# Reordering a four-layer image kernel: the last three blocks, attention in rounds of eight, and the first stage's orders

## The chip, the cores and the metric

The kernel runs on one core of a Trainium2 chip. The metric is the device time of one execution in microseconds (us); the time before is 2684.59 us, the median of three runs (2683.01 to 2685.78). All data are float32. The engines of the core are TensorE (PE, with PEld for its weight loads), VectorE (DVE), ScalarE (ACT), GpSimd (POOL) and SyncE (SP), which issues the DMAs.

## The reference

Four layers follow one another on `x`, 4 images of 512 channels and 64 x 64 pixels:

```python
# layer 0: attention over the 4096 pixels, 64 channels each for key, query, value
t = einsum('oc,bchw->bohw', w_qkv, x)                 # key_, query, value = thirds of t
attn = softmax(einsum('bdk,bdq->bkq', key_, query), axis=1)
x = scale * einsum('oc,bchw->bohw', w_out, einsum('bdk,bkq->bdq', value, attn)) + x
# layer 1: 1x1, 3x3 and 1x1 convolutions, weights mixed from 8 experts per image
rw = sigmoid(x.mean(axis=(2, 3)) @ router_w.T + router_b)
x = relu(bn3(conv(relu(bn2(conv(relu(bn1(conv(x, rw.w1))), rw.w2))), rw.w3)) + x)
# layer 2: linear attention with softplus features
Q, K, V = softplus(Wq x + bq), softplus(Wk x + bk), Wv x + bv
x = x + gamma * (Q (K V)) / (Q . (sum(K) + EPS))
# layer 3: two projections, one scanned along rows and then columns, gating the other
g, s = split(w_proj x + b_proj)
s = ds_cumsum(ds_cumsum(s, discount, axis=2), discount, axis=3)   # y_t = d*y_{t-1} + x_t
x = x + gamma * g * sigmoid(s)
```

## The kernel before, in words

**Layout.** An image is held as four pairs of pixel blocks (`NPAIR` = 4), each pair 128 partitions x 4 channel groups x 1024 pixels, in `xs[0]` to `xs[3]`; a fifth place (`places[NPAIR]`) serves as scratch. The images are worked one after the other: `layer0` to `layer3` for `b` in 0 to 3. SBUF and PSUM tiles come from pools with a number of buffers per tag: pairs of PSUM banks (`pair_psum`, tag `s`) have 3 buffers, single banks (`bank`, tag `acc`) 2, `four` 6, `block` 7. A new tile waits until the buffer that it takes has been read for the last time.

**What sets the order.** TensorE's instructions keep the order of the program everywhere (`manual_schedule` for PE around the loop over images). In the first stage VectorE and ScalarE keep it too, in the attention loop ScalarE alone, and in layer 3 VectorE and ScalarE. Where an engine is not named, a planner orders its instructions by the dependencies and its own estimates. The DMAs are all issued by SP.

**First stage of layer 0 (`Projections`).** Keys and queries of two pairs at a time come from a scheme with seven products instead of eight, each of them two accumulating matmuls per half (four pairs of matmuls in the trace). Steps are named in the strings that `steps` returns. A digit is a product: 1, 6, 7, 4 accumulate in one bank `y` (kq), 2 and 3 and 5 in a pair `zy` (kqz); product 3 writes the half of `zy` that 5 began. `seed` copies `y` after product 1 into `zy`, `e2` and `e3` copy `y` after 6 and 7 into SBUF (ScalarE), so that the next product in `y` waits for that copy. `c11` makes four copies of `zy` into the keys (ScalarE, L290), `c22` adds `zy` and `e3` into the queries (VectorE, L326), `c21` copies and `c12` adds (VectorE, L324, L318). `k` copies keys of the pair that `c12` made to the other half of the partitions (ScalarE, L290). `t5`, `t6`, `n5` and so on are differences of `x` (VectorE, L252, two instructions each): `t` for this pair of pairs, `n` for the next one, which are the terms of products 5, 6, 7 and 4. `v0` to `v3b` are the products for the values (`vv`, L260), `cp` copies these (L266), `tr` turns them on TensorE (L273) and copies the result on VectorE (L277). Image 0 has a string of its own, since its `x` is still being loaded: `wqkv_sb`, the parameters and then the blocks of `x` are the first DMAs on SP's queue, the other weights follow, and GpSimd scales two of them (L119, L120). At the head of `layer0` a preload of the exponential's activation table stands on ScalarE (L342).

**Attention.** 128 steps per image: 4 blocks of queries (`pr`), 32 blocks of keys each (`kt`). `scores(i)` is two pairs of matmuls into a pair of banks (L365), an exponential on ScalarE into one of twelve ring buffers (L368) and an addition on VectorE that sums the exponentials (`acc`, L371 and L373). `values(i)` is two pairs of matmuls from the ring buffer (L380). The loop goes by groups of six: scores of group g, then what is due of `late` (at most two entries), then values of group g - 1; in the first group there are no values, so its scores and those of the second follow each other, with `key_copies` and, in image 0, the transposes of `router_of_values` (with a copy on VectorE, L173) in between. `late` holds, for a finished block of queries, `sums` (den on TensorE, L396; a reciprocal, a product and two reductions on VectorE) and, for the first two blocks, four `out_step`s: `y` on TensorE (L424) into a pair of banks, `add_out` on VectorE (L429). The last den is in group 21, before the values of step 124. `pool` adds ScalarE work in eight of the groups (L442).

**Layer 3.** Eight tiles per image: 4 pairs by 2 pairs of channel groups. A tile has two blocks, `Sums` (the scanned projection) and `Gates` (the gate), each of seven products with the same scheme (`x` a single bank, `zy` a pair; L919). A loop over i takes `s` = sums of tile i, `g` = gates of tile i - 1, and `l` = the scans of the sums of tile i - 1, in the interleaved order of the tuples `steps`; `first_steps` serves i = 0, `last_steps` i = 8, where only the gates of tile 7 are left. `rows` scans along rows (VectorE, two instructions, L952), `turn` transposes within the partition (ScalarE, L958), `columns` adds the carry and scans (VectorE, L965, L969), `sigmoid` ends it (ScalarE, L975), `d` sets the factors of the next column scan (ScalarE, L885). `seed` and `copy_out` are ScalarE's copies as above (L924, L928). In `Gates`, `first` and `third` multiply a half tile (VectorE, L980, L987), `fourth` and `second` add and multiply (L983, L988, L992, L993); `third` and `second` end with `add_x`, which adds `x` over 1024 columns (L998) and issues one write of 512 KB on SP (L999). Between the blocks stand parts of the next image's first stage (`t`, `v`, `x`), where there is a next image.

Of the kernel before, what the change touches and what calls it, by code (L numbers as in the profile page):

```python
# [15 lines left out]
P = 128  # L16
# [20 lines left out]
RING = 12  # L37

# [7 lines left out]
def unshifted(ctx: ExitStack, tc: tile.TileContext, fits, x, wqkv_t, wout_t, router_t,  # L46
# [165 lines left out]
    class Projections:  # L212
# [16 lines left out]
        def steps(self, b):  # L229
            first = "v1 cp01 5 1 seed v2 t6 t4 n5 6 n6 e2 2 7 e3 c11 c22 tr01 n7 4 c21 3 c12 n4"  # L230
            if b == 0:
                first = "zero v0 1 seed t5 v1 cp01 t6 5 2 t7 t4 6 e2 v2 7 e3 c11 c22 tr01 n5 n6 n7 4 c21 3 c12 n4"
            return first.split(), "5 1 seed k v3a 6 e2 2 v3b cp23 7 e3 c11 c22 tr23 4 c21 3 c12".split()
# [105 lines left out]
    def layer0(b, xs, pro):  # L339


        tc.keep_in_program_order(nc.scalar.preload_act_table_set("natural_log_exp_and_others"))  # L342
# [6 lines left out]
        with tc.manual_schedule(engines={mybir.EngineType.DVE, mybir.EngineType.Activation}):  # L349
            pro.sum_weights()  # L350
            for pair, steps in zip(((0, 1), (2, 3)), pro.steps(b)):
                pro.products(xs, pair, steps, key, qry, vt)
        ringx = places[NPAIR].rearrange("p i (h n) -> p i h n", h=2)
# [89 lines left out]

        groups = [range(i, min(i + RING // 2, NPAIR * NT)) for i in range(0, NPAIR * NT, RING // 2)]
        late = []
        with tc.manual_schedule(engines={mybir.EngineType.Activation}):
            for g, group in enumerate(groups):
                for i in group:
                    scores(i)
                if 1 < g < 2 + 2 * KC:  # L450
                    pool(NPAIR - 2 + (g - 2) // KC, (g - 2) % KC)
                if g == 0:
                    pro.key_copies()
                    if b == 0:
                        router = router_of_values()
                    continue
                for _ in range(2):
                    if late and late[0][0] < g:
                        late.pop(0)[1]()
                for n, i in enumerate(groups[g - 1]):  # L460
                    if g == len(groups) - 1 and n == 4:
                        inverse_sums(NPAIR - 1)
                    pr = values(i)
# [4 lines left out]
                if b == 0 and g == 1:  # L468
                    router()
        assert not [t for t in late if t[0] < len(groups) - 1], late  # L470
# [16 lines left out]
        for i in groups[-1]:  # L487
            values(i)
# [378 lines left out]
    def layer3(b, xs, value_product, value_add, left, weights, wcq):  # L867
# [109 lines left out]
        class Gates(Block):  # L977
            def first(self):
                s = self.half(0, 0)
                nc.vector.scalar_tensor_tensor(s, self.zy[:, 0, :], self.bias[0], s, ALU.add, ALU.mult)  # L980

            def fourth(self):
                nc.vector.tensor_tensor(self.e[3], self.zy[:, 1, :], self.e[3], ALU.add)  # L983

# [549 lines left out]
```

## Time and profile before

| | |
|---|---|
| median of 3 runs | 2684.59 us (2683.01 to 2685.78) |
| profiled execution | 2685.98 us, its span 2684.2 us |
| TensorE busy | 2648.0 us, 99% of the span |
| VectorE busy | 2013.3 us, 75% |
| ScalarE busy | 1314.3 us, 49% |
| GpSimd busy | 12.1 us |
| DMA | 115.16 MB, mean 43 GB/s |
| first scores of images 0 to 3 | 57.30, 722.78, 1386.39, 2050.00 us |

The profile is one execution taken by the hardware profiler; times count from the start of its span. Idle time on an engine that is not the one that sets the pace costs nothing by itself. TensorE's matmuls are pipelined: two that use different halves of the array start within 0.01 us of each other, so pairs are what is counted here, and their spacing (0.43 us for 512 columns) tells more than their duration (about 0.6 us). The profile's stated idle time before an instruction counts from the end of the one before. The granted clock is the share of full speed that TensorE was given.

### The profile page before, as it was taken

Reading aid. Unit: us, or ns where it says so; the run is one execution under the profiler, and the core shown is the slowest. Engines: PE = TensorE matmul, PEld = TensorE weight load, DVE = VectorE, ACT = ScalarE, POOL = GpSimd, SP = SyncE. Lnnn points to the kernel's source line nnn. Section 1 sums busy time; section 2 is a strip of 40 time slices with the busy share of each in tenths; the row PEclk is TensorE's granted clock in tenths of the full one; section 3 lists DMA queues with packets and bytes.
Section 4 is the critical chain, followed back from the end, with each engine's and each line's share of the span. In section 5 each row is a group of like instructions: output and inputs, shape, how many; then the busy total and the mean of one; then the engine's idle time right before and its main releaser. Section 6 shows DMA issues by size and latency. Waiting matters only on the chain.

```text
span 2684.2 us, 25782 instructions
## 1 busy us (share of the span) xinstructions
PE 2648.0 (99%) x10048; PEld 1112.5 (41%) x10048; DVE 2013.3 (75%) x2270; ACT 1314.3 (49%) x1510; POOL 12.1 (0%) x26
## 2 busy tenths in 40 slices
PE   8999999999999999999999999999999999999998
PEld 2333364344333346434433334543443333554443
DVE  5688766788778876688877778668886787856787
ACT  3654353545565535345456553535555645363545
POOL 1000000000000000000000000000000000000000
PEclk9999999999999999999999999999999999999999
DMA  5000210021200021002220002101121000210011
GB/s 191 1 1 1 102 32 1 16 110 71 87 1 1 1 102 32 1 29 97 79 79 1 0 1 102 32 1 63 63 94 63 0 1 1 102 32 1 32 47 48
DMA packets 34594, 115.16 MB, mean 43 GB/s; under 512 B 2976, under 2 KB 12192, under 8 KB 32928
## 3 DMA queue, kind: packets, MB, share of 16 engines
q1 hardware_dynamic: 34464, 113.43, 11.4%
q8 instruction: 81, 1.33, 0.2%
q14 instruction: 49, 0.40, 0.1%
HBM read 79.86 MB, written 33.55 MB: 42 GB/s over the span
## 4 chain that ended last, share of the span: by engine, by line
PE 90%; DVE 5%; ACT 4%; issue 1%; DMA 0%; SPq 0%; DVEq 0%; ACTq 0%
PE av L380 17%; PE s L365 16%; PE sx L919 14%; PE zy L919 10%; PE z L663 4%; PE c L638 4%; PE c L566 4%; PE c L615 3%; PE wv L837 2%; PE y L424 2%; PE g L739 2%; PE xtr L724 2%; PE vv L260 2%; PE c2e L615 2%; PE kqz L304 1%; PE kq L304 1%
## 5 line engine op out<-in xcount | busy, mean ns | idle before, releaser
L365 PE MATMUL s<-qv,key 64*128 64x512 f32 x2048 | 463.9, 598 | 4.3 <-ACT x L368 3.1
L373 DVE TENSOR_TENSOR acc<-acc,ring 128x1024 f32<-128x1024 f32 x312 | 381.6, 1223 | 97.4 <-ACT ring L368 69.5
L368 ACT ACTIVATE ring<-s 128x1024 f32<-128x1024 f32 x336 | 317.1, 1038 | 211.0 <-PE s L365 211.0
L380 PE MATMUL av<-ring,qv 128*64 128x512 f32 x1344 | 304.5, 595 | 0.0
L365 PEld LDWEIGHTS s<-qv,key 64*128 64x128 f32 x2048 | 189.1, 186 | 276.2 <-issue 173.6
L373 DVE TENSOR_TENSOR acc<-acc,x 128x1024 f32<-128x1024 f32 x168 | 205.5, 1223 | 99.8 <-ACT x L368 86.6
L368 ACT ACTIVATE x<-s 128x1024 f32<-128x1024 f32 x176 | 172.0, 1041 | 181.9 <-PE s L365 181.9
L919 PE MATMUL sx<-t,x 128*128 128x512 f32 x512 | 238.1, 599 | 1.4 <-ACT e L928 0.8
L380 PEld LDWEIGHTS av<-ring,qv 128*64 128x64 f32 x1344 | 93.2, 137 | 198.7 <-issue 198.7
L380 PE MATMUL av<-x,qv 128*64 128x512 f32 x704 | 167.1, 597 | 0.0
L924 ACT COPY zy<-sx 128x512 f32<-128x512 f32 x64 | 36.5, 570 | 265.9 <-PE sx L919 256.3
L969 DVE TENSOR_TENSOR_SCAN t<-x,t 128x512 f32<-128x512 f32 x128 | 149.1, 1209 | 1.5
L919 PEld LDWEIGHTS sx<-t,x 128*128 128x128 f32 x512 | 94.6, 190 | 132.6 <-issue 121.1
L958 ACT COPY t<-s 128x1024 f32<-128x1024 f32 x64 | 127.5, 1992 | 41.9 <-DVE s L952 41.4
L952 DVE TENSOR_TENSOR_SCAN s<-wc,s 128x512 f32<-128x512 f32 x128 | 145.9, 1201 | 0.0
L928 ACT ACTIVATE e<-sx,prm_sb 128x512 f32<-128x512 f32 x128 | 86.9, 686 | 107.0 <-PE sx L919 107.0
L975 ACT ACTIVATE s<-t 128x1024 f32<-128x1024 f32 x64 | 125.6, 1988 | 12.1 <-DVE t L969 12.0
L919 PE MATMUL sx<-t,wq 128*128 128x512 f32 x256 | 117.0, 597 | 2.1 <-ACT e L928 2.1
L919 PE MATMUL zy<-t,wq 128*128 128x512 f32 x256 | 118.2, 602 | 0.0
L919 PE MATMUL sx<-x,wq 128*128 128x512 f32 x256 | 117.1, 595 | 0.0
L919 PE MATMUL zy<-x,x 128*128 128x512 f32 x256 | 116.2, 594 | 0.0
L663 PE MATMUL z<-x,wqk_sb 128*64 128x512 f32 x512 | 115.8, 597 | 0.0
(228 smaller groups left out, 3445.8 us busy)
## 6 DMA issues: line engine op xcount, KB each, us to landing
out_dram<-s SPq DMA_DIRECT2D x64, 512.0 KB, 2.6
x<-in_x_dram SPq DMA_DIRECT2D x14, 2048.0 KB, 8.7
ex<-in_packed_dram SPq DMA_DIRECT2D x4, 2048.0 KB, 7.5
ex<-in_experts_dram SPq DMA_DIRECT2D x4, 2048.0 KB, 7.8
wq<-in_wproj_t_dram SPq DMA_DIRECT2D x32, 256.0 KB, 5.1
ex<-in_packed_dram SPq DMA_DIRECT2D x4, 1536.0 KB, 6.2
ex<-in_experts_dram SPq DMA_DIRECT2D x4, 1536.0 KB, 6.8
x<-in_packed_dram SPq DMA_DIRECT2D x4, 1536.0 KB, 8.2
```

What stands on the lines that cost most here:

```text
L365: nc.tensor.matmul(s[:, h, :], key[r, kt * P:(kt + 1) * P], qry[r, pr * NB:(pr + 1) * NB], start=True, stop=True)
L368: nc.scalar.activation(p, s, AF.Exp)
L373: nc.vector.tensor_tensor(accs[pr], accs[pr], p, ALU.add)
L380: nc.tensor.matmul(avs[pr][h * D:(h + 1) * D, :], vt[:, kt, :], ring[i % RING][:, h, :], start=kt == 0, stop=kt == NT - 1)
L566: nc.tensor.matmul(y[:, h, :], wc[:, kc, :], xs[pr][:, kc, h * NB:(h + 1) * NB], start=kc == 0, stop=kc == KC - 1)
L615: nc.tensor.matmul(y[:, lo - a:hi - a], u, v[:, lo:hi], start=dy == 1, stop=dy == 2)
L663: nc.tensor.matmul(z[h * D:(h + 1) * D, i, :], wqk_sb[:, kc, w * D:(w + 1) * D], xs[pair[i]][:, kc, h * NB:(h + 1) * NB], start=kc == 0, s ...
L919: nc.tensor.matmul(y, w[:, c, self.kind, self.j * P:(self.j + 1) * P], v[:, c, :], start=c == 0 and k in (1, 5), stop=c == 1, skip_group_c ...
L952: nc.vector.tensor_tensor_scan(self.half(i, h), along[:, self.j + 2 * i, :], self.half(i, h), 0.0, ALU.mult, ALU.add)
L958: nc.scalar.copy(self.t[i].rearrange("p (w r) -> p w r", w=W), self.s[i].rearrange("p (r w) -> p w r", w=W))
L969: nc.vector.tensor_tensor_scan(th, down[:, i, :], th, 0.0, ALU.mult, ALU.add)
L975: nc.scalar.activation(self.s[i].rearrange("p (r w) -> p w r", w=W), tw, AF.Sigmoid)
```

## The change

Image 3's last round of layer 3 (i = 7) takes its steps from a new tuple `end_steps`, in which the sums and scans of tile 7 (`s`) come first, the gates of tile 6 (`g`) next to them, and the gates of tile 7 (`h`) in the same round; the loop then ends, and `last_steps` is not used for that image. The gates of tile 7 (`last`) write their outputs as four quarters of 512 columns, 256 KB, each after its own `add_x`; in `last_steps` the order of the last three steps is first, second, third. In attention the loop goes by rounds of eight scores; values follow until all but four of the steps are done, and what is due of `late` stands after the values. `key_copies` and the router's transposes move to the second round, the router's products to the third. The last den stands before the values of step 121. In the first stage `c22` stands before `c11` in all strings, in image 0's string also `n5` before both, and the preload of the activation table comes after the first pair of pairs.

```diff
@@ -35,6 +35,7 @@
 RING = 12
+ROUND = 8
@@ -227,10 +228,10 @@
-            first = "v1 cp01 5 1 seed v2 t6 t4 n5 6 n6 e2 2 7 e3 c11 c22 tr01 n7 4 c21 3 c12 n4"
+            first = "v1 cp01 5 1 seed v2 t6 t4 n5 6 n6 e2 2 7 e3 c22 c11 tr01 n7 4 c21 3 c12 n4"
             if b == 0:
-                first = "zero v0 1 seed t5 v1 cp01 t6 5 2 t7 t4 6 e2 v2 7 e3 c11 c22 tr01 n5 n6 n7 4 c21 3 c12 n4"
-            return first.split(), "5 1 seed k v3a 6 e2 2 v3b cp23 7 e3 c11 c22 tr23 4 c21 3 c12".split()
+                first = "zero v0 1 seed t5 v1 cp01 t6 5 2 t7 t4 6 e2 v2 7 e3 n5 c22 c11 tr01 n6 n7 4 c21 3 c12 n4"
+            return first.split(), "5 1 seed k v3a 6 e2 2 v3b cp23 7 e3 c22 c11 tr23 4 c21 3 c12".split()
@@ -339,7 +340,6 @@
-        tc.keep_in_program_order(nc.scalar.preload_act_table_set("natural_log_exp_and_others"))
@@ -350,6 +350,8 @@
                 pro.products(xs, pair, steps, key, qry, vt)
+                if pair[0] == 0:
+                    tc.keep_in_program_order(nc.scalar.preload_act_table_set("natural_log_exp_and_others"))
@@ -441,33 +443,32 @@
             xm = xs[pr][:, kc, :]
             nc.scalar.activation(xm, xm, AF.Copy, accum_out=pool_acc[:, kc, pr:pr + 1])
 
-        groups = [range(i, min(i + RING // 2, NPAIR * NT)) for i in range(0, NPAIR * NT, RING // 2)]
-        late = []
+        late, done = [], 0
         with tc.manual_schedule(engines={mybir.EngineType.Activation}):
-            for g, group in enumerate(groups):
-                for i in group:
+            for g in range(NPAIR * NT // ROUND):
+                for i in range(g * ROUND, (g + 1) * ROUND):
                     scores(i)
                 if 1 < g < 2 + 2 * KC:
                     pool(NPAIR - 2 + (g - 2) // KC, (g - 2) % KC)
-                if g == 0:
+                if g == 1:
                     pro.key_copies()
-                    if b == 0:
-                        router = router_of_values()
-                    continue
-                for _ in range(2):
-                    if late and late[0][0] < g:
-                        late.pop(0)[1]()
-                for n, i in enumerate(groups[g - 1]):
-                    if g == len(groups) - 1 and n == 4:
+                while done < (g + 1) * ROUND - (RING - ROUND):
+                    if done == NPAIR * NT - 7:
                         inverse_sums(NPAIR - 1)
-                    pr = values(i)
+                    pr = values(done)
+                    done += 1
                     if pr is not None:
                         late.append((g, lambda pr=pr: sums(pr)))
                         if pr < NPAIR - 2:
                             late += [(g + 1, lambda pr=pr, m=m: out_step(pr, m)) for m in range(KC)]
                 if b == 0 and g == 1:
+                    router = router_of_values()
+                if b == 0 and g == 2:
                     router()
-        assert not [t for t in late if t[0] < len(groups) - 1], late
+                for _ in range(2):
+                    if late and late[0][0] <= g:
+                        late.pop(0)[1]()
+        assert not late
 
 
         pooled = small.tile([P, KC], F32, tag="pooled", name=f"pooled_{b}")
@@ -484,7 +485,7 @@
 
         pr = NPAIR - 1
         ex4 = load_experts(b, 4, 3, bigp, "big")
-        for i in groups[-1]:
+        for i in range(done, NPAIR * NT):
             values(i)
         ex7 = load_experts(b, 7, 3, xpool, "x")
         wcq = bigp.tile([P, NPIECE + 1 + 4 * NPAIR, P], F32, tag="big", name=f"wc_{b}")
@@ -975,28 +976,45 @@
                 nc.scalar.activation(self.s[i].rearrange("p (r w) -> p w r", w=W), tw, AF.Sigmoid)
 
         class Gates(Block):
+
+            last = False
+
             def first(self):
                 s = self.half(0, 0)
                 nc.vector.scalar_tensor_tensor(s, self.zy[:, 0, :], self.bias[0], s, ALU.add, ALU.mult)
+                if self.last:
+                    self.add_x(0, 0)
 
             def fourth(self):
                 nc.vector.tensor_tensor(self.e[3], self.zy[:, 1, :], self.e[3], ALU.add)
+                if self.last:
+                    self.multiply(1, 3)
+                    self.add_x(1, 1)
 
             def third(self):
                 s = self.half(1, 0)
                 nc.vector.scalar_tensor_tensor(s, self.x, self.bias[1], s, ALU.add, ALU.mult)
-                nc.vector.tensor_tensor(self.half(1, 1), self.half(1, 1), self.e[3], ALU.mult)
-                self.add_x(1)
+                if self.last:
+                    self.add_x(1, 0)
+                else:
+                    self.multiply(1, 3)
+                    self.add_x(1)
 
             def second(self):
                 nc.vector.tensor_tensor(self.e[2], self.zy[:, 1, :], self.e[2], ALU.add)
-                nc.vector.tensor_tensor(self.half(0, 1), self.half(0, 1), self.e[2], ALU.mult)
-                self.add_x(0)
-
-            def add_x(self, i):
-                m, s = self.j + 2 * i, self.s[i]
-                nc.vector.scalar_tensor_tensor(s, s, col(GAM3), xs[self.pr][:, m, :], ALU.mult, ALU.add)
-                nc.sync.dma_start(out[b, m * P:(m + 1) * P, self.pr * 2 * NB:(self.pr + 1) * 2 * NB], s)
+                self.multiply(0, 2)
+                self.add_x(0, 1 if self.last else None)
+
+            def multiply(self, i, k):
+                nc.vector.tensor_tensor(self.half(i, 1), self.half(i, 1), self.e[k], ALU.mult)
+
+            def add_x(self, i, h=None):
+                m = self.j + 2 * i
+                n0, n1 = (0, 2 * NB) if h is None else (h * NB, (h + 1) * NB)
+                s = self.s[i][:, n0:n1]
+                nc.vector.scalar_tensor_tensor(s, s, col(GAM3), xs[self.pr][:, m, n0:n1], ALU.mult, ALU.add)
+                start = self.pr * 2 * NB
+                nc.sync.dma_start(out[b, m * P:(m + 1) * P, start + n0:start + n1], s)
 
 
 
@@ -1014,7 +1032,17 @@
                        ("s3", "s second"))
         last_steps = (("g5", "l rows 1", "l rows 0"), ("g1", "g seed", "v 0"), ("g6", "g copy_out 2", "l turn 1"), ("g2",),
                       ("g7", "g copy_out 3", "l columns 1", "g fourth", "l turn 0", "l columns 0", "l sigmoid 1",
-                       "l sigmoid 0", "v 2"), ("g4",), ("g3", "x", "g third", "g first", "g second"))
+                       "l sigmoid 0", "v 2"), ("g4",), ("g3", "x", "g first", "g second", "g third"))
+
+        end_steps = (("s1", "s seed", "l rows 1", "l rows 0"), ("g1", "l turn 1", "g seed"),
+                     ("s6", "s copy_out 2", "l columns 1"), ("s2", "l turn 0", "s first"),
+                     ("s7", "s copy_out 3", "l columns 0", "l sigmoid 1"), ("s5", "s fourth"),
+                     ("s4", "s third", "d", "s rows 1", "l sigmoid 0"), ("g5",),
+                     ("s3", "s second", "s turn 1", "s rows 0"), ("g6", "g copy_out 2"),
+                     ("g2", "s turn 0", "s columns 1"), ("h1", "h seed", "s columns 0"),
+                     ("g7", "s sigmoid 1", "g copy_out 3", "g first", "g fourth"), ("h6", "h copy_out 2"),
+                     ("h2", "s sigmoid 0", "h first"), ("g4", "g third"), ("g3", "g second"),
+                     ("h7", "h copy_out 3"), ("h5", "h fourth"), ("h4", "h third"), ("h3", "h second"))
         pro = None
         ys = [(pr, m) for pr in range(1, NPAIR) for m in range(KC)]
         nxt = []
@@ -1030,11 +1058,16 @@
             last = None
             for i in range(len(tiles) + 1):
                 who = {"l": last, "s": Sums(1, i) if i < len(tiles) else None, "g": Gates(0, i - 1) if i else None}
+                if b == B - 1 and i >= len(tiles) - 1:
+                    if i == len(tiles):
+                        break
+                    who["h"] = Gates(0, i)
+                    who["h"].last = True
                 made = None
-                for step in first_steps if i == 0 else steps if who["s"] else last_steps:
+                for step in first_steps if i == 0 else end_steps if "h" in who else steps if who["s"] else last_steps:
                     for what in step:
                         name, *args = what.split()
-                        if what[0] in "sg" and what[1:].isdigit():
+                        if what[0] in "sgh" and what[1:].isdigit():
                             if who[what[0]]:
                                 who[what[0]].product(int(what[1:]))
                         elif name in who:
```

## The prediction

> **What bounds the kernel now.** I read the page first (busy shares, the chain that ended last), then the busy time by stretches, TensorE's waits, and the timeline where TensorE is not full.
>
> ```profile
> PE 2648.0 (99%) x10048; PEld 1112.5 (41%) x10048; DVE 2013.3 (75%) x2270; ACT 1314.3 (49%) x1510; POOL 12.1 (0%) x26
> PE 90%; DVE 5%; ACT 4%; issue 1%; DMA 0%; SPq 0%; DVEq 0%; ACTq 0%
> ```
>
> TensorE bounds it: 36.2 us of 2684.2 are idle, and the change removes no matmul. So it can win only idle time, time in which matmuls are stretched, and what follows the last matmul. The stretches (columns: us, then busy of PE, PEld, DVE, ACT, POOL, the granted clock, DMA) say where that is:
>
> ```profile
> 0.00:20.00 20.00, 15.29 (x52) 4.29 (x54) 10.10 (x32) 4.42 (x6) 0.91 (x8) 1.00 0.90 330
> 20.00:60.00 40.00, 34.66 (x158) 11.71 (x156) 23.34 (x23) 11.17 (x19) 8.41 (x2) 0.96 0.44 154
> 80.00:700.00 620.00, 618.92 (x2322) 262.61 (x2319) 473.46 (x532) 304.70 (x346) 0.69 (x4) 1.00 0.12 45
> 2634.00:2684.20 50.20, 36.97 (x87) 15.61 (x85) 36.62 (x43) 23.27 (x21) 0.00 (x0) 0.93 0.16 65
> ```
>
> Image 0's first stage and the last block are open; the long middle is full. TensorE's waits:
>
> ```profile
> PE kqz L304 <- DVE qv L326: 6.1, 8, 0.8
> PE kqz L304 <- DVE ring L252: 3.8, 1, 3.8
> PE s L365 <- ACT x L368: 3.1, 3, 1.0
> PE s L365 <- DVE wot_sb L173: 1.2, 1, 1.2
> ```
>
> Below, "product" is four pairs of matmuls, 1.72 us (kq 688.72 to vv 690.44), one step of scores or values is two pairs, 0.86.
>
> **Order of c22 and c11.** In the first stage c22 (L326, VectorE) reads e3, ready at 28.99, but starts at 31.28, after the last of c11's four key copies on ScalarE; product 3 waits for it.
>
> ```profile
> 31.28 0.69 DVE L326 TENSOR_TENSOR qv<-kqz,e 128x512 f32<-128x512 f32 x1 [8.48 <-ACT key L290]
> 33.09 5.67 DVE L252 TENSOR_TENSOR ring<-x,x 128x1024 f32<-128x1024 f32 x2
> 37.77 3.02 PE L304 MATMUL kqz<-ring,wqkv_sb 128*64 128x512 f32 x8 [3.80 <-DVE ring L252]
> ```
>
> Emitted first, c22 waits for e3 alone: in images 1 to 3, product 4 starts at 700.59 and 3 could at 702.31 instead of 703.30, 0.99 each. Two halves of three images: **-6.0**. c11 moves back by c22's 0.69 at most; its readers, the scores, come over 2 us after it.
>
> **Image 0's first stage.** Now n5 also stands ahead of c22. The last block of x is issued at 8.70 and lands 19.8 later, at 28.5. So n5 runs 28.5 to 31.0 (two of 1.23), c22 to 31.7, and product 3 starts at 31.76 instead of 32.03 (0.27). Product 5 follows at once, where it waited 4.02 for n5 (33.75 to 37.77). The granted clock fell after that idle: products 5 and 1 took 5.25 (37.77 to 43.02) instead of 3.44, 1.81 more. With the second half's 0.99 that is 7.09. Given back: GpSimd's scaling of wv (32.83 to 38.27), which stretched n5's two to 5.67, now meets n6: n6 32.9 to 38.6, n7 to 41.3 (2.76 in its row), c21, c12 to 43.4 (1.40). Behind c12 on ScalarE stand k (1.34) and e2 (0.58): 45.25. Product 7 overwrites what e2 reads; its slot is 31.76 + 7 x 1.72 = 43.8, so it waits 1.5. Net **-5.6**: first scores at 51.7 instead of 57.3. Bounds: 3.0 if GpSimd slows n7 like n6, 7.1 if k is not late.
>
> **Table load.** In images 1 to 3 it delays vsb's copies and so product vv.
>
> ```profile
> 688.41 1.28 ACT L342 ACT_TABLE_LOAD   x1
> 689.71 1.07 ACT L266 COPY vsb<-vv 128x512 f32<-128x512 f32 x2
> ```
>
> vv starts at 690.83 against a slot at 690.44: 0.39 x 3 = **-1.2**. Behind c11 the load is covered: c11 ends at 703.2 at the latest, the seed after it can start at 708.7, so 5.5 us hide 1.28. The row has the next copy 1.30 after the load's start. The Trainium skill, ScalarE: Activation LUTs, What ACT_TABLE_LOAD costs, speaks against moving a load among copies: it adds a drain, 2.66 us in all, which this row does not show. Inside the cover the sum is the same by both.
>
> **Rounds of eight.** Three effects, and one new cost each in two places.
> - The long first run. Before, twelve scores came first, with key copies behind the sixth on ScalarE: 1.31 lost (730.51 to 731.82) in images 1 to 3, 1.48 in image 0 behind wot_sb (64.96 to 66.44). Now eight, then four values; copies and router come a round later, behind values. Nine scores ran without a wait:
>
> ```profile
> 722.78 8.00 PE L365 MATMUL s<-qv,key 64*128 64x512 f32 x36
> 731.82 2.94 PE L365 MATMUL s<-qv,key 64*128 64x512 f32 x12 [1.04 <-ACT x L368]
> ```
>
> Gain **-5.4**.
> - Fewer switches between scores and values:
>
> ```profile
> 1503.75 5.42 PE L365 MATMUL s<-qv,key 64*128 64x512 f32 x24
> 1509.10 3.65 PE L380 MATMUL av<-ring,qv 128*64 128x512 f32 x16
> 1514.40 1.13 PE L365 MATMUL s<-qv,key 64*128 64x512 f32 x4
> ```
>
> A round of six takes 10.65; 24 pairs of 0.4295 are 10.31; 0.34 is the switch there and back. 21 such per image become 16: 5 x 0.34 x 4 = **-6.8**.
> - The last den. It needs the sum of the last exponentials, and VectorE adds more slowly than scores come:
>
> ```profile
> 279.77 5.21 DVE L373 TENSOR_TENSOR acc<-acc,ring 128x1024 f32<-128x1024 f32 x4 [2.78 <-ACT ring L368]
> 294.67 3.36 DVE L399 RECIPROCAL rec<-den 128x512 f32<-128x512 f32 x1 [1.69 <-PE den L396]
> ```
>
> Pitch 1.33, first add 2.23 after the round's start (277.54). In the last round eight adds end at 2.23 + 7 x 1.33 + 1.22 = 12.8; den stands behind eight scores (7.07) and five values (4.34), at 11.4. Before, den had no wait. 1.4 x 4 = **+5.7**; bounds 0 and 2 a piece. The seven values behind den still cover the reciprocal (3.36).
> - out_step before scores. Before, two y's stood between scores and values, and 10 us of values hid their add_out (L429, 1.28). Now the next scores follow: two of three score buffers hold y's. In the round after sums, VectorE runs late: reciprocal to stat 5.06 (138.32 to about 143.85 + 0.6, less the addition between), then eight adds, free 30.7 after the round with den began; y0 is done at 30.05. add_out ends at 32.0 and 33.2; the second and third score stand at 31.7 and 32.9 and wait 0.36 and 0.35. The next two y's cost 0.05. 0.75 x 2 blocks x 4 images = **+6.0**; bounds 0 (adds done in time) and 14 (both rounds like twice the first).
>
> **The last blocks.** From the first product of tile 7's sums (2634.08; everything counted from there), 21 products stand in both versions, 36.06 us. Before, VectorE's last addition ends 44.9 and the span 5.2 later:
>
> ```profile
> 2676.98 0.69 DVE L993 TENSOR_TENSOR s<-s,e 128x512 f32<-128x512 f32 x1
> 2677.70 1.28 DVE L998 SCALAR_TENSOR_TENSOR s<-s,prm_sb,x 128x1024 f32<-128x1024 f32 x1
> ```
>
> After, by the rows' durations (scan 1.14, turn 2.00, columns 2.6 a pair, sigmoid 1.96, copies 0.57 to 0.69): tile 6's rows run 2.85 to 7.4; ScalarE does turn 1 (5.2 to 7.2), g seed, s copy_out 2 (to 8.5), so s7 waits for it from 6.87: 1.7 new. Then s rows 1 ends 17.0, s rows 0 20.3, s columns 1 23.0, s columns 0 25.55, s sigmoid 0 28.55. All g and h products find their copies done; the last, h3, ends at 37.8. But h first stands on VectorE ahead of g third and waits for that sigmoid. Behind it: h first and a half add_x 1.4, g third 2.6, g second 2.7, h fourth 2.1, h third 1.4, h second 2.2: end at 40.9, 4.1 earlier than 44.9. g third and g second, ready at 27.4 and 31.1, are what is queued behind the waiting h first.
>
> Outputs: SP issues two writes more, 0.33 each, well before the end. The last is 256 KB instead of 512 KB, whose median landing is 2.6 us: gain between 0 and 1.3, I take 0.6. Last blocks: **-4.7**; bounds 1.5 (s sigmoid 0 later by 3) and 6.5.
>
> **Images 0 to 2, last block.** Its order becomes first, second, third: first waits for sigmoid 0 (ScalarE, to 688.39), where third could begin at 686.15. VectorE stands 2.2 and third, second's followers and SP's writes move back as much, so it ends at 696.3 instead of 694.1. Next on it is n5, which waits for x until 696.09 and is wanted by product 5 at 705.07: **0**; uncovered it would be 2.2 x 3 = 6.6.
>
> **Sum.** -6.0 - 5.6 - 1.2 - 5.4 - 6.8 + 5.7 + 6.0 - 4.7 = -18.0 us. The profiled execution took 2685.98 (span 2684.2 and 1.8 around it), 1.4 over the median of 2684.59; the difference put on the median gives 2666.6, say 2667.
>
> **Rivals.**
> 1. No new waits in attention: VectorE's order is left to the planner there, and the adds keep up. 18.0 + 11.7 gives 29.7: 2655. Against it: eight adds at 1.33 cannot end before 12.8. 12%.
> 2. c22 goes on waiting for ScalarE, so the change doesn't do what its order says: 7 x 0.99 + 0.27 are lost, 2674. Against: the copies now stand behind it. 8%.
> 3. The tail gives nothing (VectorE as late as before) and y's cost double: 18.0 - 4.7 - 6.0 = 7.3, 2677. For it: VectorE is full from 28.6 to the end. 15%.
> 4. Slower: the planner puts one addition of the next round ahead of each add_out. It needs that round's first exponential (2.23) and then 1.33 and 1.28: the second score waits 4.0 in each of 16 y rounds, +64 in place of +6.0: 2725. It decides from 24.0/16 = 1.5 us a round. Against: y is done 3 us before that addition could start. 7%.
>
> **How the numbers follow.** The forecast holds 55% (its own range 2661 to 2673); 3% lies between it and the old time. What a measurement tells apart is 0.2%, 5.4 us. Faster: 55 + 12 + 8 + 13 of rival 3 = 88%; same 2 + 3 = 5%; slower 7%. The range reaches from rival 1 to rival 3: 2656 to 2678.
>
> **What would show it.** L304's waits on L326 go to one; the 3.80 and the 0.5 clock go; first scores near 51.7; score runs of 32 matmuls, no wait inside; den waiting 1.4 four times on L373; scores waiting on L429; a wait of 1.7 on e at s7; last VectorE end 41 after tile 7's first product. Wrong if scores wait in every round, or VectorE's order in attention differs.

## The result and the profile after

The kernel after takes 2678.17 us (median of six runs, 2676.54 to 2678.64); the kernel before, run beside it, 2684.32 (2683.01 to 2685.78). The ratio is 0.9976 [0.9963, 0.9989]: 6 us shorter, where 18 were forecast, and 0.2 above the upper end of the range (2678). The profiled execution took 2678.12 us, its span 2676.2; that is 8.0 under the span of before, because the profiled execution of before was 1.7 over its median. The stages below are compared between these two spans.

The page of after, its first part and the share of the chain by engine:

```profile
PE 2643.2 (99%) x10048; PEld 1114.9 (42%) x10048; DVE 2016.3 (75%) x2272; ACT 1314.3 (49%) x1510; POOL 12.9 (0%) x26
PE 81%; DVE 11%; ACT 3%; issue 2%; DMA 1%; DVEq 0%; SPq 0%; ACTq 0%
```

TensorE is idle for 33.0 us (2676.2 - 2643.2) instead of 36.2; the other 4.8 us came out of its busy time, with the same number of matmuls. The chain runs through VectorE for twice the share it had, which says that it passes through more waits for other engines, not fewer. The stretches, columns as before (us, then busy of PE, PEld, DVE, ACT, POOL, granted clock, DMA share, GB/s); the last begins with the first product of tile 7's sums:

```profile
20.00:60.00 40.00, 37.41 (x177) 13.21 (x175) 26.02 (x26) 16.43 (x25) 9.23 (x2) 1.00 0.45 156
80.00:700.00 620.00, 616.81 (x2320) 263.53 (x2318) 475.54 (x537) 305.71 (x348) 0.69 (x4) 1.00 0.12 45
2628.90:2676.20 47.30, 36.91 (x87) 15.62 (x85) 36.93 (x45) 22.82 (x21) 0.00 (x0) 0.96 0.18 69
```

Image 0's first stage is fuller and its clock is whole; the long middle is 2.1 us emptier; the last blocks are 2.9 us shorter. TensorE's waits (total us, times, longest):

```profile
PE kqz L305 <- ACT key L291: 8.4, 8, 1.6
PE den L398 <- DVE acc L375: 5.0, 4, 1.2
...
PE sx L920 <- ACT e L929: 3.6, 9, 1.4
...
PE zy L920 <- ACT s L938: 0.5, 1, 0.5
```

The first line is the result in short. The eight waits of product 3 (`kqz`) for c22 (VectorE) are gone, and eight waits of the same product for c11's key copies (ScalarE) stand in their place, 8.4 us instead of 6.1. The waits of the scores are gone from the list, den has the wait that was forecast, and two waits of layer 3 are new or longer.

By stage, from the starts of TensorE's rows (first scores, first product of `mix`, first product of layer 3) in both timelines:

| us | before | after | difference | forecast |
|---|---|---|---|---|
| start to first scores of image 0 | 57.30 | 53.53 | -3.8 | -5.6 |
| layer 3 to next first scores, images 1 to 3 | 256.69, .67, .68 | 256.51, .71, .74 | -0.1 | -7.2 |
| attention, four images | 247.41, 245.56, .55, .55 | 247.14, 245.21, .22, .22 | -1.3 | -0.5 |
| layer 3 of image 3 to the end | 227.27 | 224.43 | -2.8 | -4.7 |
| span | 2684.2 | 2676.2 | -8.0 | -18.0 |

Seven of the ten missing microseconds are in one row, the second. The first row is of one execution each: with before's first stage, first scores come at 56.39 to 57.30 (before, rounds_alone and last_blocks_alone), with after's at 51.92 to 54.70 (after and four of the runs below).

### The profile page after: what moved, and what is told of

The parts are those of the page before. It is cut to its first block, busy times and chain, and to the rows that moved or that the text cites. A ratio compares the mean times of both kernels' runs of the same rounds, so it can differ in the third digit from the quotient of the medians.

```text
span 2676.2 us, 25813 instructions
## 1 busy us (share of the span) xinstructions
PE 2643.2 (99%) x10048; PEld 1114.9 (42%) x10048; DVE 2016.3 (75%) x2272; ACT 1314.3 (49%) x1510; POOL 12.9 (0%) x26
## 4 chain that ended last, share of the span: by engine, by line
PE 81%; DVE 11%; ACT 3%; issue 2%; DMA 1%; DVEq 0%; SPq 0%; ACTq 0%
PE av L382 14%; PE sx L920 14%; PE s L367 13%; PE zy L920 10%; DVE acc L375 4%; PE z L664 4%; PE c L639 4%; PE c L567 4%; PE c L616 3%; PE wv L838 2%; PE g L740 2%; PE xtr L725 2%; PE y L426 2%; PE c2e L616 2%; PE kqz L305 1%
## 5 line engine op out<-in xcount | busy, mean ns | idle before, releaser
L382 PE MATMUL av<-x,qv 128*64 128x512 f32 x704 | 159.6, 595 | 0.0
L920 PE MATMUL zy<-x,wq 128*128 128x512 f32 x256 | 115.9, 592 | 0.0
```

The lines of the kernel that those rows point to most:

```text
L382: nc.tensor.matmul(avs[pr][h * D:(h + 1) * D, :], vt[:, kt, :], ring[i % RING][:, h, :], start=kt == 0, stop=kt == NT - 1)
L920: nc.tensor.matmul(y, w[:, c, self.kind, self.j * P:(self.j + 1) * P], v[:, c, :], start=c == 0 and k in (1, 5), stop=c == 1, skip_group_c ...
```

## Experiments

Two theories for that row. A: c11 moved onto the path. `zy` is one tile of two halves; c11 reads half 0, c22 reads half 1, product 3 writes half 1. If every user of the tile waits for the one emitted before it, product 3 waits for whichever of c22 and c11 comes last in the string, and the swap only exchanges one for the other. B: the swap did what was forecast and the attention's new waits or the moved table load took the gain away. The timeline of after, image 2, speaks for A (timelines here show the rows that the text speaks of; others between them are left out):

```profile
1358.30 0.59 ACT L313 COPY e<-kq 128x512 f32<-128x512 f32 x1 [2.85 <-PE kq L305]
1359.13 0.69 DVE L327 TENSOR_TENSOR qv<-kqz,e 128x512 f32<-128x512 f32 x1
1359.85 2.35 ACT L291 COPY key<-kqz 64x512 f32<-64x512 f32 x4 [0.97 <-DVE qv L327]
1362.22 1.28 ACT L354 ACT_TABLE_LOAD   x1
1362.26 1.94 PE L305 MATMUL kqz<-x,kqw 128*64 128x512 f32 x8 [1.12 <-ACT key L291]
```

c11 starts 0.03 after c22 ends (1359.82), although both only read `zy`; product 3 starts 0.06 after c11 ends (1362.20), although c11 reads the other half. Ten runs separate the parts; each is compared with the kernel before on its own chip.

| run | us | before | ratio, 95% interval |
|---|---|---|---|
| swap_alone | 2685.53 | 2683.80 | 1.0005 [0.9996, 1.0014] |
| c11_behind_2 | 2668.78 | 2683.80 | 0.9941 [0.9928, 0.9955] |
| rounds_alone | 2683.10 | 2683.80 | 0.9995 [0.9985, 1.0004] |
| last_blocks_alone | 2681.16 | 2683.80 | 0.9988 [0.9979, 0.9997] |
| den_later | 2672.62 | 2685.01 | 0.9956 [0.9942, 0.9969] |
| late_before_values | 2675.58 | 2685.01 | 0.9965 [0.9951, 0.9979] |
| flag_early | 2678.54 | 2685.01 | 0.9980 [0.9971, 0.9989] |
| all_four | 2658.52 | 2685.01 | 0.9902 [0.9887, 0.9917] |
| n5_back | 2677.11 | 2685.42 | 0.9971 [0.9960, 0.9982] |
| halves | 2678.70 | 2685.42 | 0.9977 [0.9967, 0.9987] |

**swap_alone.** The kernel before with c22 ahead of c11 in the three strings.

```diff
-n5 6 n6 e2 2 7 e3 c11 c22 tr01 n7
+n5 6 n6 e2 2 7 e3 c22 c11 tr01 n7
-t4 6 e2 v2 7 e3 c11 c22 tr01 n5
+t4 6 e2 v2 7 e3 c22 c11 tr01 n5
-7 e3 c11 c22 tr23
+7 e3 c22 c11 tr23
```

> The kernel before with c22 ahead of c11 in the three strings of the first stage, nothing else. Theory A (every reader of the tile zy stands in one chain, and product 3 waits for the last of them): product 3 no longer waits for c22 (0.77 us idle, eight times) but for c11's fourth copy, which now comes after c22; in the changed kernel that wait is 8.4 us in eight, so the time is 0 to 3 us longer than before. Theory B (the prediction's: product 3 waits only for c22, and the gain was lost elsewhere): 6 to 7 us shorter than before, and no wait of product 3 on ScalarE.

It gains nothing. TensorE's waits of this kernel (us, times, longest), and its timeline in image 1:

```profile
PE kqz L304 <- ACT key L290: 11.2, 8, 3.2
```

```profile
694.89 0.59 ACT L312 COPY e<-kq 128x512 f32<-128x512 f32 x1 [2.85 <-PE kq L304]
695.87 0.68 DVE L326 TENSOR_TENSOR qv<-kqz,e 128x512 f32<-128x512 f32 x1
696.59 2.35 ACT L290 COPY key<-kqz 64x512 f32<-64x512 f32 x4 [1.10 <-DVE qv L326]
698.99 1.94 PE L304 MATMUL kqz<-x,kqw 128*64 128x512 f32 x8 [1.25 <-ACT key L290]
```

The chain c22, c11, product 3 is there without any other part of the change, so B isn't needed. c22 also starts 0.39 after e3 has ended (695.48): it stands behind n6 on VectorE, and n5 ahead of that waits for `x`. In images 2 and 3 `x` lands later still and the wait grows to 3.2. An `x` that lands late now holds up product 3; in before, product 3 starts 2.71 after product 4 in all three images, since c22 waits for c11 longer than for n6. So images 1 to 3 lose 4.8 us (layer 3 to first scores 257.3, 258.3, 259.2 against 256.7), and image 0 wins 4.8 (first scores at 52.50), the two of a size.

**c11_behind_2.** The kernel after with c11 right behind product 2, which ends half 0; c22 is then the last user before product 3.

```diff
-n5 6 n6 e2 2 7 e3 c22 c11 tr01
+n5 6 n6 e2 2 c11 7 e3 c22 tr01
-t6 5 2 t7 t4 6 e2 v2 7 e3 n5 c22 c11 tr01
+t6 5 2 c11 t7 t4 6 e2 v2 7 e3 n5 c22 tr01
-6 e2 2 v3b cp23 7 e3 c22 c11 tr23
+6 e2 2 c11 v3b cp23 7 e3 c22 tr23
```

> The changed kernel with c11 emitted right behind product 2, which completes the half of zy that c11 reads, so that c22 is the last reader ahead of product 3. Theory A: the waits of product 3 on the key copies (8.4 us) go, and e3 comes up to 0.6 us later in the first half of images 1 to 3, where the copies are still under way; 5 to 8 us shorter than the changed kernel, 11 to 14 shorter than before. Theory B (product 3 waits for something else): within 1.5 us of the changed kernel.

By the ratios it is 9.4 us shorter than after, a little more than expected. No wait of `kqz` for a copy is left; what is late next is a copy out of `kq` (ScalarE, L313), 1.2 us in three waits. Image 0 in its timeline:

```profile
22.57 2.35 ACT L291 COPY key<-kqz 64x512 f32<-64x512 f32 x4 [2.42 <-PE kqz L305]
...
30.28 1.94 PE L305 MATMUL kq<-ring,wqkv_sb 128*64 128x512 f32 x8
30.32 0.68 DVE L327 TENSOR_TENSOR qv<-kqz,e 128x512 f32<-128x512 f32 x1
32.05 1.89 PE L305 MATMUL kqz<-x,kqw 128*64 128x512 f32 x8
```

Product 3 follows product 4 without a wait. Layer 3 to first scores falls to 254.73 in each of images 1 to 3, 1.96 less than before in image 1. Product 3 starts 1.77 after product 4 instead of 2.71 and is 0.05 shorter itself, in both halves: the two waits of 0.99 that the forecast counted. Beside them the wait of `vv` is gone (0.46), and the late copy out of `kq` costs as much (0.48). First scores of image 0 come at 50.80. In sum the forecast of this part (-6.0, -5.6 and -1.2) is nearly what this kernel gets (5.9 and 6.5), and the string that was to bring it isn't the one in the change. Theory A is shown.

**n5_back.** The kernel after with n5 of image 0 back behind tr01.

```diff
-e3 n5 c22 c11 tr01 n6 n7 4
+e3 c22 c11 tr01 n5 n6 n7 4
```

> The kernel after with n5 put back behind tr01 in image 0's string, nothing else. If moving n5 ahead is what closed image 0's first stage (the prediction's reading), the wait of 3.8 before product 5 comes back and the first scores are 3 to 4 us later than 53.53, the time 3 to 4 longer than after. If the swap of c22 and c11 did it alone and n5 only holds c22 back (what the swap alone suggests: first scores at 52.50), the first scores come at about 52.5 and the time is 0.5 to 1.5 shorter than after. Images 1 to 3 are the same as after.

First scores come at 52.18; the time is 1 us under after's, which the two intervals don't tell apart. The wait of 3.8 doesn't come back, so the swap opens image 0's first stage by itself, as in swap_alone (first scores at 52.50).

```profile
29.34 0.69 DVE L327 TENSOR_TENSOR qv<-kqz,e 128x512 f32<-128x512 f32 x1 [6.98 <-ACT e L313]
...
31.15 2.35 DVE L253 TENSOR_TENSOR ring<-x,x 128x1024 f32<-128x1024 f32 x2
32.48 1.94 PE L305 MATMUL kqz<-x,kqw 128*64 128x512 f32 x8 [0.89 <-ACT key L291]
33.42 5.79 DVE L253 TENSOR_TENSOR ring<-x,ring 128x1024 f32<-128x1024 f32 x2
```

c22 starts right behind e3 (29.32), c11 and product 3 follow; n5 is done at 33.5, before product 5 needs it, and the next pair of differences takes 5.79 beside GpSimd's scaling (32.77 to 39.86). Product 4 itself starts between 29.04 and 30.36 from one execution to the next, so what n5 ahead of c22 costs is read from product 4's start to product 3's: 2.83 here and 2.84 in swap_alone, and with n5 in front 3.56 (after), 3.27 (halves), 3.74 (den_later), 2.84 (flag_early) and 4.24 (late_before_values). n5 waits for the last block of `x`, so it costs between nothing and 1.4 there. In late_before_values more came behind it:

```profile
33.38 2.61 PE L305 MATMUL kqz<-x,kqw 128*64 128x512 f32 x8 [2.31 <-ACT key L291]
35.77 2.96 PE L305 MATMUL kqz<-ring,wqkv_sb 128*64 128x512 f32 x8
38.56 1.89 PE L305 MATMUL kq<-x,wqkv_sb 128*64 128x512 f32 x8
```

After the wait of 2.31 the granted clock was 0.50 (35 to 37 us), and products 3 and 5 took 5.18 together instead of 3.48 in after. A wait of 3.17 before product 3 in image 3 of swap_alone was followed by no such fall (granted clock 1.00), so the length of the wait alone doesn't decide it.

**rounds_alone.** The kernel before with the attention loop of after and nothing else.

```diff
-        groups = [range(i, min(i + RING // 2, NPAIR * NT)) for i in range(0, NPAIR * NT, RING // 2)]
-        late = []
+        late, done = [], 0
...
-        for i in groups[-1]:
+        for i in range(done, NPAIR * NT):
```

> The kernel before with attention in rounds of eight alone. Theory (the four terms of the prediction stand, and cancel): per image 1.2 us of the long first run and 1.7 us of switches gained, 1.4 at the last den and 1.2 at the scores behind y's lost, so 1 to 2 us shorter over four images; den waits on VectorE's additions about 1.2 us four times. Rival (attention is where the gain went, by more than the trace's waits show): at or above the time before.

Attention is 0.33 shorter in images 1 to 3 and 0.61 in image 0, 1.6 in all, as expected; the time can't be told from no change. Den waits for the additions as in after, 5.0 us in four.

**den_later.** The kernel after with the last den two steps of values later.

```diff
-                    if done == NPAIR * NT - 7:
+                    if done == NPAIR * NT - 5:
```

> The changed kernel with the last den before the values of step 123 instead of 121. Theory: eight additions end 12.8 us after the last round starts, and two steps of values (1.72 us) more put den's slot at 13.1, so its wait (1.2 us of idle, 1.4 against its slot, four times) goes: 5 to 6 us shorter than the changed kernel, about 2672.5; five steps of values (4.3 us) then still cover the reciprocal (3.36). Rival: the reciprocal ends behind the values and the first y waits for it: no gain.

The wait is gone and attention takes 243.77 in images 1 to 3, 1.45 less than after (1.43 in image 0): 5.8 in four images, the forecast's term of 5.7.

**late_before_values.** The kernel after with what is due of `late` between scores and values, as before.

```diff
+                for _ in range(2):
+                    if late and late[0][0] < g:
+                        late.pop(0)[1]()
                 while done < (g + 1) * ROUND - (RING - ROUND):
...
-                for _ in range(2):
-                    if late and late[0][0] <= g:
-                        late.pop(0)[1]()
```

> The changed kernel with what is due of late between scores and values again (one round later for sums), the rounds of eight kept. Theory: the short waits of the second and third score behind y's (0.38 and 0.29 us, 1.2 per image) go and no wait takes their place, since 7 us of values hide the additions: 4 to 5 us shorter than the changed kernel, about 2673.5. Rival (these small waits are only the price of changing from values to scores, and stay): within 1.5 us of the changed kernel.

Attention falls by 1.26 per image, as expected; the time falls by less (2.6 against 4 to 5). In this kernel's profile the rest is in the first stages: product 3's waits for c11 came out longer (10.1 us in eight, against 8.4), and the clock fell in image 0, as told under n5_back. In after, the cost shows in the timeline of a y round as scores that take 7.35 from their start (802.32) to that of the values, instead of 7.07 in a round without y's (757.39 to 764.46):

```profile
800.50 1.99 PE L426 MATMUL y<-o,wout_sb 64*128 64x512 f32 x8
801.78 1.28 DVE L431 SCALAR_TENSOR_TENSOR x<-y,prm_sb,x 128x1024 f32<-128x1024 f32 x1
802.32 7.42 PE L367 MATMUL s<-qv,key 64*128 64x512 f32 x32
809.67 7.09 PE L382 MATMUL av<-ring,qv 128*64 128x512 f32 x32
```

**last_blocks_alone.** The kernel before with `end_steps`, the quarters and the new order of `last_steps`.

```diff
-                for step in first_steps if i == 0 else steps if who["s"] else last_steps:
+                for step in first_steps if i == 0 else end_steps if "h" in who else steps if who["s"] else last_steps:
```

> The kernel before with the last blocks' order and the quarter outputs alone. Theory: VectorE's last addition 3 us earlier against the first product of tile 7, the write after it no shorter, so 2 to 4 us shorter than before. Rival (the changed kernel's tail owes its gain to the earlier start of everything before it): within 1 us of before.

The last part is 2.5 shorter (224.73 against 227.27), and layer 3 to first scores 0.43 to 0.45 shorter in images 1 to 3, which the forecast had put at nothing: the waits of `vv` for `vsb` (0.7 in three) are gone without the table load having moved.

**flag_early.** In after, the last matmul is a small count (`cnt`, at 2667.48), and branches follow (TensorE's from 2670.09, VectorE's at 2670.47); in before the count ran at 2661.64, 10 us ahead of the last matmul (2671.69). Here that test stands ahead of layer 3 of image 3.

```diff
             parts = layer2(b, xs, *convs)
+            if b == B - 1:
+                check_sums()
             xs, pro = layer3(b, xs, *parts)
```

> The changed kernel with the closing test of the sums (the matmul cnt and what leads to it) issued ahead of layer 3 of image 3 instead of behind it. Theory: in the changed kernel the engines branch at 2670 to 2671 and the instructions fetched then share the DMA engines with the last output, which lands 3.6 us after its issue where the three quarters before it take 2.0; with the branch off TensorE's and VectorE's end that landing becomes 2.0 to 2.6: 1 to 1.6 us shorter than the changed kernel. Rival (the last write takes 3.6 us whatever the branch does): within 0.5 us.

No gain: the last write still takes 3.8. TensorE's branch moved to 2666.97, but VectorE's stayed at 2670.75, just ahead of the last write (2670.90), so the edit took away only one of the two that it was to take.

**halves.** The kernel after with the last tile's outputs in two writes of 512 KB.

```diff
-                    who["h"].last = True
```

> The kernel after with the last tile's outputs as two halves of 512 KB again in place of four quarters. VectorE is full from tile 7's sigmoid on, and two additions over 1024 columns take 0.2 less than four over 512, but the one behind the last product is 0.6 longer: its end is -0.2 to +0.6 against after's 2670.59. If the size of the last write sets its landing, it takes 2.6 to 3.0 and the span ends within 0.6 of after or earlier. If something else on the DMA engines at that moment adds 1.6 whatever the size (the quarter took 3.63 where its like took 2.0), it takes 4.2 to 4.6 and the span is 0.6 to 1.6 longer than after's. The quarters are worth 0 to 0.6 by the first theory, 0.6 to 1.6 by the second.

Layer 3 to the end takes 225.25, 0.82 more than in after. The eight kernels with quarters take 224.30 to 224.98, so the quarters are worth 0.3 to 0.95; the times can't tell it (2678.70 against 2678.17, on different chips). VectorE's end moves by 0.6, from 3.08 to 3.68 after the start of the last matmul, as its row of 1.28 in place of 0.75 says. The landing of the last write answers neither expectation, see the last section.

**all_four.** The kernel after with the edits of c11_behind_2, den_later, late_before_values and flag_early together.

> The changed kernel with c11 behind product 2, the last den before the values of step 123, what is due of late between scores and values, and the closing test early. If the four are independent: 9.4 (measured for c11 alone) + 5.5 + 4.6 + 1.3 = 21 us shorter than the changed kernel, about 2658; if the waits taken away had covered for one another, only the largest of them, 2668.

2658.52 us, 1.0% under before [0.9887, 0.9917], and it beats after as clearly. By stage the edits add up: against after, attention is 11.2 shorter (den_later and late_before_values give 2.71 per image, 10.8), and the first stages are 8.4 shorter, as in c11_behind_2 (8.5). The expected sum of 21 held the 1.3 of flag_early, which didn't come; the spans differ by 19.4. Of TensorE's waits the largest left are those for the first `x` and in layer 3:

```profile
PE vv L261 <- DMA x<-in_x_dram: 4.0, 1, 4.0
PE sx L920 <- ACT e L929: 3.5, 9, 1.4
...
PE kq L305 <- ACT e L313: 1.2, 3, 0.4
...
PE zy L920 <- ACT s L938: 0.5, 1, 0.5
```

## Why the prediction was wrong in size

**Order of c22 and c11: the step that failed.** It read: "Emitted first, c22 waits for e3 alone: in images 1 to 3, product 4 starts at 700.59 and 3 could at 702.31", and "c11 moves back by c22's 0.69 at most; its readers, the scores, come over 2 us after it." The row that it started from was right, and so was the size of the stall: c11_behind_2 won the 0.99 in each half. What was left out is that c11 has more than readers of its result: product 3 overwrites what c11 reads from, as far as the order of the tile goes, and waited for it as it had for c22. A reader moved back holds up the next writer, and the two readers of `zy` wait for each other too (0.03 between them). The same question was asked of c12, k and e2 in the next paragraph ("Product 7 overwrites what e2 reads"), not here. Forecast -6.0; in after, product 3 starts 2.84 to 3.07 after product 4 where it was 2.71 in before, 1.2 longer over the six halves.

The second rival (c22 goes on waiting) had the price of this, 7 x 0.99 + 0.27, and 2674 for it; its mechanism wasn't there, since c22 does wait for e3 alone in second halves:

```profile
1376.88 0.69 DVE L327 TENSOR_TENSOR qv<-kqz,e 128x512 f32<-128x512 f32 x1 [8.76 <-ACT e L313]
1377.60 2.35 ACT L291 COPY key<-kqz 64x512 f32<-64x512 f32 x4 [0.76 <-DVE qv L327]
1380.01 1.94 PE L305 MATMUL kqz<-x,kqw 128*64 128x512 f32 x8 [0.90 <-ACT key L291]
```

**Image 0's first stage: -5.6 forecast, -3.8 measured.** The timeline of after:

```profile
28.52 2.36 DVE L253 TENSOR_TENSOR ring<-x,x 128x1024 f32<-128x1024 f32 x2 [5.95 <-DMA x<-in_x_dram]
30.79 0.69 DVE L327 TENSOR_TENSOR qv<-kqz,e 128x512 f32<-128x512 f32 x1
...
32.85 7.32 POOL L120 TENSOR_SCALAR wv_sb<-wv_sb,prm_sb 128x2048 f32<-128x2048 f32 x1 [31.38 <-DMA bv_sb<-in_bv_dram]
33.92 1.94 PE L305 MATMUL kqz<-x,kqw 128*64 128x512 f32 x8 [1.62 <-ACT key L291]
```

n5 and c22 ran when they were forecast to (28.5, about 31.0), the stall of 3.80 and the granted clock of 0.50 behind it (39 to 42 us in before) are gone. Product 3 started at 33.92 instead of the forecast 31.76 (2.16 lost): 1.8 by c11, and the rest because product 4 itself started at 30.36 instead of 29.32. Its second wait didn't shrink by 0.99, by c11 again; the 1.5 of e2 behind k and c12 didn't come. -5.6 + 2.16 + 0.99 - 1.5 is -3.95, near the -3.77 of this execution; others with the same first stage differ from it by up to 1.6. The forecast took the gain for n5's; n5_back shows that it was the swap's.

**Table load: -1.2 forecast, nothing of it kept.** The waits of `vv` for `vsb` did go, and product 3's longer waits took up as much: the row of images 1 to 3 is -0.1 in all. last_blocks_alone shows that the order of the last steps removes these waits too, so the forecast's 0 for that edit was wrong in the kernel before (-0.44 per image) and the two gains would not have added up. What the load's move does by itself wasn't run.

**Rounds of eight: right, one term in its sum only.** In image 1 the gaps of the attention add up to -1.21 for the long first run (forecast -1.3), -1.76 for the switches (-1.7), +1.40 for den (+1.4) and +1.16 for the y's (+1.5), together -0.4 against -0.34 of the stage. The y's came to their sum by other parts: the forecast had 0.71 in the first of the two rounds with y's and 0.05 in the second, and scores to values is longer in both (7.35 and 7.26 instead of 7.07). den_later (1.45) and late_before_values (1.26) measure the two costs by themselves. The rival that had no new waits here is out: eight additions don't keep up with eight scores.

```profile
276.35 5.21 DVE L375 TENSOR_TENSOR acc<-acc,ring 128x1024 f32<-128x1024 f32 x4 [3.56 <-ACT ring L370]
281.67 5.21 DVE L375 TENSOR_TENSOR acc<-acc,x 128x1024 f32<-128x1024 f32 x4
286.93 1.08 PE L398 MATMUL den<-acc,ones 128*64 128x512 f32 x4 [1.24 <-DVE acc L375]
```

The additions end at 286.88, and den starts 0.05 later. The slower rival (an addition put ahead of add_out) didn't come: add_out at 801.78 runs before the round's first addition (804.45).

**Last blocks: -4.7 forecast, -2.8 measured; two terms mis-sized.** Everything counted from tile 7's first product (2628.95):

```profile
2637.36 1.98 PE L920 MATMUL sx<-t,x 128*128 128x512 f32 x4 [1.39 <-ACT e L929]
2639.07 0.69 ACT L938 ACTIVATE s<-zy,prm_sb 128x512 f32<-128x512 f32 x1
2639.82 1.98 PE L920 MATMUL zy<-t,wq 128*128 128x512 f32 x4 [0.47 <-ACT s L938]
2658.15 0.75 DVE L984 SCALAR_TENSOR_TENSOR s<-zy,prm_sb,s 128x512 f32<-128x512 f32 x1 [1.79 <-ACT s L976]
2669.84 0.75 DVE L1015 SCALAR_TENSOR_TENSOR s<-s,prm_sb,x 128x512 f32<-128x512 f32 x1
```

s7 waits 1.39 for the copy (forecast 1.7) and h first waits for the sigmoid, as forecast. Not forecast: s5 waits 0.47 for `s first`, which reads the other half of the same pair, the step that failed in the first stage once more. h first starts at 29.20 instead of 28.55, and VectorE ends at 41.64 instead of 40.9. The second term is the last write: the span ends 5.64 after VectorE, 0.44 later than before, where 0.6 less was taken and 0 was the bound. (44.9 less 40.9 is 4.0, and four times 1.4 is 5.6: the forecast's 4.1 and 5.7 are a tenth off, which changes nothing.)

**The rivals and the range.** The third rival's 2677 is nearest to the time, by none of its mechanism: the tail gave 2.8 of 4.7, and the y's cost 1.2 per image, not twice the forecast. The direction was right (the chance for faster was 0.88). The range was too narrow because its upper end rested on the tail and the y's, and the largest term of all, the order of c22 and c11, was bounded only by a rival in which nothing of the edit took effect, and not by another copy taking c22's place.

## What to carry to other kernels

When a reader of a buffer is moved back in the order, ask who writes that buffer next: in this kernel a wait for "the buffer" was a wait for its last reader in the order written, even where the two touch different halves, and a swap of two readers then only changed the name in the list of waits. The cure here was to emit each reader as soon as its half is finished (c11 behind product 2), not to argue which of the two is urgent. Where a stage's gain is absent, look first at the same stall under a new name.

## What the runs showed of the hardware

**The last write of after is slow at either size.** The DMA view of after for single writes, the one before the last and then the last, and of halves for its last:

```profile
out_dram<-s SPq DMA_DIRECT2D x1, 256.0 KB, 2.0
```

```profile
q14 instruction: 7, 0.06, 3.9%
q8 instruction: 2, 0.03, 2.9%
out_dram<-s SPq DMA_DIRECT2D x1, 256.0 KB, 3.6
```

```profile
out_dram<-s SPq DMA_DIRECT2D x1, 512.0 KB, 3.6
```

In after, 256 KB took 2.0 us for each quarter but the last, 512 KB a median of 2.6; the last write took 3.6 in both, and between 3.5 and 4.2 in the other kernels with quarters. In all of them the DMA engines also fetch instructions in that window (queues q8 and q14, 0.08 to 0.09 MB, 0.04 in flag_early and all_four), and no instruction packets stand beside the quarter that took 2.0. In before, whose last 512 KB took 3.0, the fetch in that window was smaller:

```profile
q14 instruction: 3, 0.02, 1.6%
out_dram<-s SPq DMA_DIRECT2D x1, 512.0 KB, 3.0
```

In flag_early one quarter earlier took 3.7, beside a fetch that had moved there with TensorE's branch, and the last kept its 3.8 beside the rest of the fetch. That fits a write held up by instruction fetch, though in flag_early and all_four half the fetch stands beside a write that is as long; no run took all of the fetch away from the last write, so the cause stays open. The Trainium skill, DMA: Bandwidth & Descriptors, Anatomy of one DMA — SWDGE (gpsimd) path, gives a fixed 2.0 us and the bytes over 436e3; by it 256 KB are an estimated 2.6 us. The rows here, of another path, have 2.0 for an undisturbed quarter, and the measurement decides.

**Two halves of a pair are waited for as one.** Product 3 waits 0.9 us and more for a copy from the other bank of its pair. The Trainium skill, PSUM — Partial Sum Buffer, PSUM bank collisions raise a hardware error, reports two engines on different banks as running clean, so by that page the chip would not ask for this wait. Taking the wait away alone, or giving each half a tile of its own, wasn't tried; c11_behind_2 shows only that the order written decides which copy is waited for.
